# Two attention layers and a mixture of experts: the buffers of the second attention moved, its close dealt out differently among VectorE, ScalarE and GpSimd

## The chip, the cores and the metric

The kernel runs on one core of one Trainium2 chip. The metric is the device time of one execution in microseconds, lower is better. Beside the times there is one execution recorded by the hardware profiler. A core has a matrix engine (TensorE, PE in the profile, with its weight loads as PEld), three elementwise engines (VectorE is DVE, ScalarE is ACT, GpSimd is POOL) and SyncE (SP), which here only starts DMA transfers. Each engine works through its own instructions in order, and they meet at semaphores. PE's clock is granted by a throttle and is shown as a share of full speed.

## What is computed

Four rows of 1024 tokens, 256 numbers each, pass through a first layer of gated attention and a low-rank feed-forward part, then through a second attention and a mixture of experts (8 experts, each takes its 1024 best tokens); each of the four has a normalised input and a normalised output that is added to the stream:

```python
def _L1_attn_ref(x, w_qkv, w_out, b_out, gamma, beta):
    B, S, D, H = (4, 512, 256, 16)
    HD = D // H
    def kernel_func(q, k):
        scores = jnp.einsum('bhqd,bhkd->bhqk', q, k) / jnp.sqrt(jnp.asarray(HD, q.dtype))
        w = jax.nn.relu(scores)
        return w / (jnp.sum(w, axis=-1, keepdims=True) + KERN_EPS)
    ...
    attn = kernel_func(q, k)
    out = jnp.einsum('bhqk,bhkd->bhqd', attn, v)
    out = out.transpose(0, 2, 1, 3).reshape(Bx, Sx, D)
    out = out @ w_out + b_out
    y = x + out
    mu = jnp.mean(y, axis=-1, keepdims=True)
    var = jnp.var(y, axis=-1, keepdims=True)
    return (y - mu) * jax.lax.rsqrt(var + LN_EPS) * gamma + beta
...
x = x + _layernorm(_L0_attn_ref(_layernorm(x, axis=-1), ...), axis=-1)
x = x + _layernorm(_L0_ffn_ref(_layernorm(x, axis=-1), ...), axis=-1)
x = x + _layernorm(_L1_attn_ref(_layernorm(x, axis=-1), ...), axis=-1)
x = x + _layernorm(_L1_ffn_ref(_layernorm(x, axis=-1), ...), axis=-1)
```

The change concerns the second attention, and the end of the first layer where it hands over.

## The kernel before

**Stages.** The first layer (gated attention with its feed-forward part) takes lines 481 to 1080. The tokens are eight blocks `t` of 512 (half rows), each of four tiles of 128 (`NJ`). `add_normalized` gives the steps that normalise a block's result `y` and add it to the residual `xs[t]`; its `apply` runs on ScalarE (L577) and ends with an add on GpSimd (L588). During the last block of this stage, row 0 of the second attention is already projected. The second attention is lines 1090 to 1638, and the mixture of experts follows.

**Score steps.** The second attention is a hand-written loop over rows `b`, half rows `qh`, four groups `g` of four heads, and eight key tiles `kt`: 256 steps. `scores` issues eight matmuls for four heads: two into single PSUM tiles (`s`, three buffers, shared with the side work) and two into a pair tile (`d`, two buffers). ScalarE applies relu to the two singles (L1493), VectorE to the pair (L1498), into a tile `w` of SBUF with three buffers. In the last half row, which is worked in two halves, ScalarE takes the pair in every fourth step (`all_on_act`, L1496). `weigh` (L1510) multiplies the `w` of the step before the last by the values, one step in a loop iteration, accumulating into `po`. When a group ends, VectorE transposes `po` into `turned` (L1563), and every second group `divide` normalises by the sum of weights (L1243 to L1253).

**Side work.** Everything else is cut into `Part`s. Each has needs (other parts, each with an age in steps that must have passed), an estimate of what it costs VectorE, ScalarE and TensorE, and sits in one of two lists. `beside` holds pieces with PE work: projections of the next row (pk, pq, pv), out projections (`pt`, L1274), transposes, gates. One is taken per step, placed ahead of or after the value matmuls. `rest` holds the elementwise parts; `go_on` deals as many as fit. For this, `late` estimates how far each engine is behind: a part adds its cost less the TensorE time that it brings, and every step subtracts an allowance (0.4 us for VectorE, 0.53 for ScalarE); a part is dealt when `late` plus its cost stays within `MOST`. GpSimd has no such estimate. The order of PE, DVE and ACT instructions is that in which this planner issues them (`manual_schedule`).

**The close of a block.** `close` runs after a half row's last group. Per pair of tiles, `project_out` makes `pt` and VectorE adds the residual (L1284) into `y`. Per tile: `stats_y` (statistics on VectorE, then rs and ms on GpSimd, L1113 to L1118), `affine` on GpSimd (three operations: L1122, L1290, L1291), statistics of the result, `shift` on ScalarE (L1295), `add` on VectorE (L1300), statistics again, and `token_rows` (GpSimd L1122 and SP DMAs). `shift` and `add` apply the outer normalisation. The next row's `normalize` (tags `a`) and the projections' last additions lie beside this.

**Buffers.** The pools of the stage are opened in the order `l1a` (work tiles: y, h, hg, oT, ...), `l1w` (the three w tiles), and lie on SBUF space which the first layer's pools have left: the w tiles lie over a work buffer of the first layer, the one that the last block's `y` uses.

**Queues.** Projected q and k go as high and low parts through DRAM: SP stores them (`q_d<-wh`, `q_d<-parts`, `k_d<-parts`), GpSimd's queue loads them back in another layout (L370 kT, L377 q). The parts are built in a list of room tiles that `next_parts` hands out in turn.

Of the kernel before, what the change touches and what calls it, by code (L numbers as in the profile page):

```python
# [74 lines left out]
def kernel(  # L75
# [146 lines left out]
    with ExitStack() as st1:  # L222
# [358 lines left out]
        def add_normalized(tag, t, y):  # L581

            r, stats, scales, shift = stats_steps(tag, y)

            def apply(i0):
                apply_on_act(y(), y(), r, i0)
                if i0:
                    nc.gpsimd.tensor_tensor(xs[t], xs[t], y(), ALU.add)  # L588

            gap = POW if t < NB - 1 else 2.0  # L590
            return [*stats, (0.0, scales), (gap, shift), (0.5, lambda: apply(0)), (0.0, lambda: apply(2))]

# [176 lines left out]
        def first_parts():  # L769

            room = iter(
                [[wh[:, c, i * TB : (i + 1) * TB] for i in range(2)] for c in range(DC)]
                + [[wk.tile([P, TB], F32, tag=tag, name="part", bufs=1) for tag in ("qk", "head3")]]
            )
            kept = list(room)

            def next_parts():
                kept.append(kept.pop(0))
                return kept[-1]

            return next_parts
# [14 lines left out]

        state = {}

        def attend(d, then=None):
# [290 lines left out]
    with ExitStack() as st3:  # L1090

        wk = st3.enter_context(tc.tile_pool(name="l1a", bufs=2))
        wts = st3.enter_context(tc.tile_pool(name="l1w", bufs=3))
        ps = st3.enter_context(tc.tile_pool(name="l1a_ps", bufs=1, space=PSUM))
# [11 lines left out]

        def scale_of(tag, src):

            st = small.tile([P, 6], F32, tag=f"st{tag}", name=f"st{tag}")
            mv = small.tile([P, 2], F32, tag=f"mv{tag}", name=f"mv{tag}")  # L1110
            ve = small.tile([P, 1], F32, tag=f"ve{tag}", name=f"ve{tag}")
            rs = small.tile([P, 1], F32, tag=f"rs{tag}", name=f"rs{tag}")
            nc.vector.bn_stats(st, src)  # L1113
            nc.vector.bn_aggr(mv, st)
            nc.vector.tensor_scalar(ve, mv[:, 1:2], EPS, None, ALU.add)  # L1115
            ms = small.tile([P, 1], F32, tag=f"ms{tag}", name=f"ms{tag}")
            nc.gpsimd.tensor_tensor(rs, ve, mhalf[:, 0:1], ALU.pow)  # L1117
            nc.gpsimd.tensor_scalar(ms, mv[:, 0:1], rs, -1.0, ALU.mult, ALU.mult)  # L1118
            return rs, ms
# [5 lines left out]
        class Part:  # L1125
# [4 lines left out]

            def __init__(self, do, needs=(), vector=0.0, scalar=0.0, tensor=0.0, when=None):
                self.do, self.needs, self.when = do, needs, when
                self.takes, self.tensor = (vector, scalar), tensor
                self.at = None
# [12 lines left out]

        STATS = {"vector": 0.72}

# [17 lines left out]
        def normalize(row, b, k):  # L1167

            h, x = row["h"][k], xs[b * BPB + k]

            def stats(i):
                return scale_of("a", x[:, i, :])

            def apply(i, rs, ms):
                scaled(h[:, i, :], x[:, i, :], rs, ms)

            return by_tile((stats, 0, STATS), (apply, 1, {}))

# [83 lines left out]
        def close(t, h, oT, tiles, at_end):  # L1262
# [3 lines left out]
            def new_y():  # L1266
                nonlocal y
                y = wk.tile([P, NJ, D], F32, tag="y", name="y", bufs=1)
                last_use["y"] = [] if at_end else [parts[4, i] for i in tiles]

# [14 lines left out]
            def stats_y(i):  # L1285
                return scale_of("b", y[:, i, :])

            def affine(i, rs, ms):
                scaled(y[:, i, :], y[:, i, :], rs, ms)
                nc.gpsimd.tensor_tensor(y[:, i, :], y[:, i, :], gam, ALU.mult)  # L1290
                nc.gpsimd.tensor_tensor(y[:, i, :], y[:, i, :], bet, ALU.add)  # L1291

# [142 lines left out]
            if at_end:  # L1435
                return [at_once]
            steps = (
                (stats_y, 0, STATS), (affine, 1, {}), (lambda i: scale_of("c", y[:, i, :]), 2, STATS),
                (shift, 1, {"scalar": 0.5}), (add, 1, {"vector": 0.48}), (stats_x, 0, STATS),
                (token_rows_and_on, 1, {}),  # L1440
            )
            parts = by_tile(*steps, tiles=tiles)
            outs, turns = [], []
            for i in tiles[1::2]:
# [3 lines left out]
                for k in (i - 1, i):  # L1448
                    parts[0, k].needs.append((outs[-1], 0))
                turns.append(  # L1450
                    Part(
                        lambda i=i: turn_gating(i - 1), [(parts[6, i], 2), *((x, 0) for x in turns[-1:])],
                        tensor=0.53, scalar=0.59,
                    )
                )
            outs[0].when = lambda: done(last_use["y"])
            parts[6, tiles[0]].when = lambda: done(last_use["hg"])
            turns[0].when = may_turn
# [8 lines left out]

        def all_on_act(row, halves, kt):

            return halves > 1 and kt // halves % 4 == 1  # L1470

        def scores(row, qh, q2, halves, g, kt):

# [18 lines left out]
            for j, sc in enumerate(singles):  # L1492
                nc.scalar.activation(w[:, j, :], sc, AF.Relu)  # L1493
            if all_on_act(row, halves, kt):

# [26 lines left out]

        late, MOST = [0.0, 0.0], (0.8, 0.2)

# [5 lines left out]

        def next_piece():

            for part in beside:
                if part.ready():
                    beside.remove(part)
                    take(part)
                    return

# [39 lines left out]

        def go_on_with_oldest():

            at = waiting.pop(0)
            if fresh[0]:
                next_piece()
            finish(*at)
            _, _, _, _, halves, g, kt, _ = at
            ended = kt == KT - halves
            if ended:
                late[0] += 0.65 / halves
            elif not fresh[0]:
                next_piece()  # L1590
            fresh[0] = ended

        for b in range(B):
            after = open_row(last=b + 2 == B) if b + 1 < B else None
            for qh in range(BPB):
# [13 lines left out]
                for q2 in range(halves):  # L1609
                    for g in range(NG):  # L1610
                        for kt in range(0, KT, halves):
                            w = scores(row, qh, q2, halves, g, kt)
                            waiting.append((row, b, qh, q2, halves, g, kt, w))
                            Part.now += 1
                            step = kt // halves
                            if step == 1 and g % 2 == 0:
                                if g == 0 and q2 == 0:
                                    fetch_queries(row, qh, 1)
                                elif g and halves == 1:
                                    fetch_queries(*((row, 1) if qh == 0 else (after, 0)), 0)  # L1620
                            on_act = 1.03 if all_on_act(row, halves, kt) else 0.0
                            for i, us in enumerate((0.4 + 1.2 * (on_act > 0), 0.53 - on_act)):
                                late[i] -= us
                            if len(waiting) > 2:
                                go_on_with_oldest()
                            go_on()
# [4 lines left out]
        while beside or rest:  # L1631
            Part.now += 1
            assert Part.now < 2000
            late[:] = [-2.0, -2.0]
            next_piece()
            go_on()
# [562 lines left out]
```

## Time and profile before

| what | value |
|---|---|
| median of 3 runs | 1552.57 us (1549.29 to 1552.65) |
| the profiled execution | 1552.29 us, its span 1550.5 us |
| mean granted TensorE clock | 0.975 |
| first layer, 0 to 421 us | PE busy 408.8, DVE 237.4, ACT 184.0, POOL 120.7 |
| second attention, 421 to 1011.5 us | PE busy 561.1 of 590.5, DVE 461.0, ACT 335.0, POOL 226.0 |
| experts, 1028 to 1550.5 us | PE busy 490.5 of 522.5, DVE 217.9, ACT 109.8, POOL 199.8 |
| relu of two singles, L1493 | 512 of 595 ns |
| relu of the pair on VectorE, L1498 | 248 of 1216 ns |
| relu of the pair on ScalarE, L1496 | 8 of 1031 ns |
| affine on GpSimd, per tile | L1122 552 ns, L1290 748, L1291 727 |
| fused two-input on VectorE, L1300 | 30 of 476 ns |

A busy time is the sum of an engine's instructions in a stretch. In a group's line the first number after the bar is busy time, the second the mean of one instruction in ns, then the idle time of the engine just before them with what ended it. In a timeline a line is start, duration, engine, line and operation, and in brackets the idle time before it and who released it. In a table of windows the columns are the stretch, its length, then busy time (and count) of PE, PEld, DVE, ACT and POOL, the granted clock, the DMA share and GB/s.

### The profile page before, as it was taken

The page shows a single profiled execution, that of the slowest core. Times are in us where ns is not written, and L with a number is a line of the kernel's source. Part 1 is how long each engine was busy: PE and PEld are TensorE (multiplying, and loading weights), DVE is VectorE, ACT ScalarE, POOL GpSimd, SP SyncE. Part 2 cuts the span into 40 slices and gives each one's busy share as a digit, 9 for nine tenths or more (in the row PEclk, how much of TensorE's full clock was granted, in tenths as well). Part 3 has the DMA queues.
Part 4 walks back from the last instruction along what each step waited for, and adds up shares of the span by engine and source line. Part 5 has one row for each costly group of instructions (what it writes and reads, how often), then busy time and mean ns, then how long its engine had stood idle before and what let it go on. Part 6 is the DMA issues. An engine that isn't in the chain of part 4 may idle for free. (4 is left out here: it accounts for less than half of the span.)

```text
span 1550.5 us, 24225 instructions
## 1 busy us (share of the span) xinstructions
PE 1474.1 (95%) x9286; PEld 789.5 (51%) x9286; DVE 928.5 (60%) x2130; ACT 636.4 (41%) x1109; POOL 549.6 (35%) x731
## 2 busy tenths in 40 slices
PE   8999999999799999999999889959999999999996
PEld 4666666666432323332323224526656765675674
DVE  5455665556467788777877878875545632222145
ACT  4244445543455555645554656722122112112142
POOL 4122333223321336333633244412425233342554
PEclk9999999999899999999999999979999999999998
DMA  9400000004313331532243211151324233233364
GB/s 216 126 1 1 1 1 0 1 1 150 112 52 123 89 110 56 157 108 90 69 143 111 91 34 54 32 164 32 79 42 114 55 73 85 59 77 77 65 166 119
DMA packets 91885, 121.58 MB, mean 78 GB/s; under 512 B 24925, under 2 KB 64250, under 8 KB 91642
## 3 DMA queue, kind: packets, MB, share of 16 engines
q1 hardware_dynamic: 70000, 73.09, 15.2%
q0 software_dynamic: 21712, 46.94, 13.2%
q8 instruction: 73, 1.20, 0.3%
q14 instruction: 42, 0.34, 0.1%
q10 hardware_dynamic: 58, 0.01, 0.0%
HBM read 66.90 MB, written 53.12 MB: 77 GB/s over the span
## 5 line engine op out<-in xcount | busy, mean ns | idle before, releaser
L1493 ACT ACTIVATE w<-sc 128x512 f32<-128x512 f32 x512 | 277.7, 595 | 162.0 <-ACT w L1493 71.0
L1498 DVE TENSOR_SCALAR w<-sc 128x1024 f32<-128x1024 f32 x248 | 300.3, 1216 | 62.2 <-PE sc L1484 49.7
L1510 PE MATMUL po<-w,vaug 128*17 128x512 f32 (+1 forms) x2304 | 275.4, 561 | 6.2 <-DVE turned L1563 6.2
L2074 PE MATMUL ph<-xT,w 128*128 128x512 f32 (+1 forms) x544 | 229.6, 574 | 0.3 <-DVE xT L2057 0.3
L2091 PE MATMUL py<-w,hid 128*128 128x256 f32 x1024 | 229.7, 380 | 0.0
L2081 ACT ACTIVATE hid<-ph,mb 128x512 f32<-128x512 f32 (+1 forms) x136 | 89.9, 662 | 340.2 <-PE ph L2074 246.7
L1484 PE MATMUL sc<-q,kT 32*128 32x512 f32 (+1 forms) x2304 | 199.9, 421 | 23.5 <-ACT w L1493 22.2
L2091 PEld LDWEIGHTS py<-w,hid 128*128 128x128 f32 x1024 | 191.7, 190 | 31.7 <-issue 6.7
L1484 PEld LDWEIGHTS sc<-q,kT 32*128 32x128 f32 x2304 | 90.1, 187 | 209.3 <-ACT w L1493 146.3
L2112 POOL DMA_INDIRECT acc_d<-y,idx x56 | 88.5, 1580 | 226.0 <-DVE y L2111 112.0
L2074 PEld LDWEIGHTS ph<-xT,w 128*128 128x128 f32 x544 | 99.7, 190 | 107.2 <-issue 98.4
L2110 DVE TENSOR_TENSOR y<-py,mb 128x256 f32<-128x256 f32 x56 | 23.5, 419 | 127.0 <-PE py L2091 113.1
L1510 PEld LDWEIGHTS po<-w,vaug 128*17 128x17 f32 x2304 | 42.0, 96 | 103.6 <-issue 74.9
L1882 POOL DMA_INDIRECT got<-tok_d,idx x64 | 66.2, 1034 | 62.5 <-DVE counts L1716 24.5
L2057 DVE COPY xT<-tp 128x512 f32<-128x512 f32 (+1 forms) x34 | 22.2, 659 | 71.7 <-PE tp L2052 64.1
L716 PE MATMUL pg<-nT,wh 128*128 128x512 f32 x128 | 61.3, 611 | 1.5 <-ACT nT L655 1.4
L838 PE MATMUL py<-wo,oT 128*128 128x256 f32 x256 | 61.9, 385 | 0.0
L732 PE MATMUL pv<-wh,nT 128*128 128x512 f32 x128 | 59.7, 592 | 0.0
L838 PEld LDWEIGHTS py<-wo,oT 128*128 128x128 f32 x256 | 47.2, 190 | 17.2 <-issue 9.6
L588 POOL TENSOR_TENSOR x<-x,y 128x1024 f32<-128x1024 f32 x14 | 32.9, 2350 | 59.9 <-ACT y L577 59.8
L1117 POOL TENSOR_TENSOR rsg<-veg,mhalf 128x1 f32<-128x1 f32 x30 | 16.6, 552 | 98.6 <-DVE veg L1115 98.5
L903 ACT ACTIVATE hid<-ph,vec 128x512 f32<-128x512 f32 x64 | 39.8, 685 | 27.5 <-PE ph L894 27.3
(303 smaller groups left out, 2060.6 us busy)
## 6 DMA issues: line engine op xcount, KB each, us to landing
q<-q_d POOLq DMA_DIRECT2D x16, 1024.0 KB
w<-in_L_ffn_W_dram SPq DMA_DIRECT2D x16, 1024.0 KB
q_d<-parts SPq DMA_DIRECT2D x48, 256.0 KB
kT<-k_d POOLq DMA_DIRECT2D x16, 512.0 KB
k_d<-parts SPq DMA_DIRECT2D x24, 256.0 KB
acc_d<-logits SPq DMA_DIRECT2D x8, 512.0 KB
q_d<-wh SPq DMA_DIRECT2D x16, 256.0 KB
tok_d<-hg SPq DMA_DIRECT2D x32, 128.0 KB
```

Of the source, the lines that this page charges most:

```text
L716: nc.tensor.matmul(pg, lhsT=wh[:, c, HID + e * P : HID + (e + 1) * P], rhs=d["nT"][:, c, :], start=(c == 0), stop=(c == DC - 1),)
L732: nc.tensor.matmul(pv, lhsT=d["nT"][:, c, i * P : (i + 1) * P], rhs=wh[:, c, 0:HID], start=(c == 0), stop=(c == DC - 1),)
L838: nc.tensor.matmul(py, lhsT=d["oT"][:, e, :], rhs=wo[:, e, :], start=(e == 0), stop=(e == EC - 1))
L1484: nc.tensor.matmul(sc[:, m * n : (m + 1) * n], lhsT=row["kT"][t][rows, r, (kt + m) * P : (kt + m + 1) * P], rhs=row["q"][qh, t][rows, r, p ...
L1493: nc.scalar.activation(w[:, j, :], sc, AF.Relu)
L1498: nc.vector.tensor_scalar(w[:, 2:4, :], pair, 0.0, None, ALU.max)
L1510: nc.tensor.matmul(po[32 * j : 32 * j + HD + 1, weighed(halves, r)], lhsT=row["v"][:, kt + m, HQ * t + 4 * r + j, :], rhs=w[:, j, m * n : ...
L1882: return nc.gpsimd.indirect_dma_start(out=dst, out_offset=None, in_=rows[:, :], in_offset=self.at_chunk(c), bounds_check=NT - 1, oob_is_er ...
L2074: nc.tensor.matmul(ph, lhsT=w1[:, c, f * P : (f + 1) * P], rhs=xT[u][:, c, h * n : (h + 1) * n], start=(c == 0), stop=(c == DC - 1),)
L2081: nc.scalar.activation(hid[:, f, h * n : (h + 1) * n], ph, AF.Gelu, bias=mb1[:, e * FC + f : e * FC + f + 1])
L2091: nc.tensor.matmul(py, lhsT=hid[:, f, i * P : (i + 1) * P], rhs=w2[:, f, :], start=(f == 0), stop=(f == FC - 1),)
L2112: scatter = nc.gpsimd.indirect_dma_start(out=acc_d[:, :], out_offset=lists[e].at_chunk(k), in_=y, in_offset=None, bounds_check=NT - 1, oob ...
```

## The change

Four things are edited.

1. **Buffers.** The pool of the w tiles is opened ahead of that of the work tiles, so the w tiles take the first addresses, where weights of the first layer lay. So that the room of the parts isn't needed longer, `next_parts` hands out its room twice and then takes tiles "h" of the next row (`next_hs`), which `open_row` uses afterwards. The last block of the first layer is applied on GpSimd by four scalings and the add (`apply_on_pool`).
2. **The close.** `stats_y` no longer makes ms. `centre` on VectorE computes (y - mean) * gam in one instruction, and `affine` is one more on VectorE, y * rs + bet; in the last row `affine` stays on GpSimd as two. `shift`, the tile's `apply` and `token_rows` must be two steps behind what they need instead of one.
3. **The planner.** `late` and `MOST` have a third entry for GpSimd, and parts carry a `pool` cost. The piece for a step is chosen before its scores are issued. When a group's end is one or two steps off, one piece that could be done is kept back.
4. **The score pair.** ScalarE takes it in every step whose piece holds PE for more than 1.5 us, and in one of eight steps of a group in the last row (one of four in the half steps).

Counted in the two instruction orders: ACT pair relus go from 8 to 63 and VectorE's from 248 to 193; VectorE gets 30 centres and 24 affines; GpSimd loses 30 scaled y, 30 msb, 30 multiplies by gam and 24 adds of bet, and gets 10 scalings. The matmuls are the same in number.

```diff
@@ add_normalized
-            gap = POW if t < NB - 1 else 2.0
-            return [*stats, (0.0, scales), (gap, shift), (0.5, lambda: apply(0)), (0.0, lambda: apply(2))]
+            def apply_on_pool():
+                for i in range(NJ):
+                    nc.gpsimd.tensor_scalar(
+                        y()[:, i, :], y()[:, i, :], r["mv"][:, i, 0:1], r["rs"][:, i : i + 1], ALU.subtract, ALU.mult
+                    )
+                nc.gpsimd.tensor_tensor(xs[t], xs[t], y(), ALU.add)
+
+            if t == NB - 1:
+                return [*stats, (0.0, scales), (0.0, apply_on_pool)]
+            return [*stats, (0.0, scales), (POW, shift), (0.5, lambda: apply(0)), (0.0, lambda: apply(2))]
@@ first_parts
-            kept = list(room)
+            kept = 2 * list(room)
 
             def next_parts():
-                kept.append(kept.pop(0))
-                return kept[-1]
+                if kept:
+                    return kept.pop(0)
+                next_hs.append(act4("h"))
+                part = next_hs[-1].rearrange("p j d -> p (j d)")
+                return part[:, 0:TB], part[:, TB : 2 * TB]
@@ pools of the second attention
+        wts = st3.enter_context(tc.tile_pool(name="l1w", bufs=3))
         wk = st3.enter_context(tc.tile_pool(name="l1a", bufs=2))
-        wts = st3.enter_context(tc.tile_pool(name="l1w", bufs=3))
@@ normalize
-            return by_tile((stats, 0, STATS), (apply, 1, {}))
+            return by_tile((stats, 0, STATS), (apply, 2, {"pool": 0.6}))
@@ close
             def stats_y(i):
-                return scale_of("b", y[:, i, :])
-
-            def affine(i, rs, ms):
-                scaled(y[:, i, :], y[:, i, :], rs, ms)
-                nc.gpsimd.tensor_tensor(y[:, i, :], y[:, i, :], gam, ALU.mult)
-                nc.gpsimd.tensor_tensor(y[:, i, :], y[:, i, :], bet, ALU.add)
+                return scale_of("b", y[:, i, :], False)
+
+            def centre(i, mean, rs):
+                nc.vector.scalar_tensor_tensor(y[:, i, :], y[:, i, :], mean, gam, ALU.subtract, ALU.mult)
+                return (rs,)
+
+            def affine(i, rs):
+                if at_last:
+                    nc.gpsimd.tensor_scalar(y[:, i, :], y[:, i, :], rs, None, ALU.mult)
+                    nc.gpsimd.tensor_tensor(y[:, i, :], y[:, i, :], bet, ALU.add)
+                else:
+                    nc.vector.scalar_tensor_tensor(y[:, i, :], y[:, i, :], rs, bet, ALU.mult, ALU.add)
...
             steps = (
-                (stats_y, 0, STATS), (affine, 1, {}), (lambda i: scale_of("c", y[:, i, :]), 2, STATS),
-                (shift, 1, {"scalar": 0.5}), (add, 1, {"vector": 0.48}), (stats_x, 0, STATS),
-                (token_rows_and_on, 1, {}),
+                (stats_y, 0, STATS), (centre, 0, {"vector": 0.48}), (affine, 1, {"pool": 1.4} if at_last else {"vector": 0.49}),
+                (lambda i: scale_of("c", y[:, i, :]), int(at_last), STATS), (shift, 2, {"scalar": 0.5}),
+                (add, 1, {"vector": 0.48}), (stats_x, 0, STATS), (token_rows_and_on, 2, {"pool": 0.6}),
             )
@@ planner
-        late, MOST = [0.0, 0.0], (0.8, 0.2)
+        late, MOST = [0.0, 0.0, 0.0], (0.8, 0.2, 0.4)
-        def next_piece():
-
-            for part in beside:
-                if part.ready():
-                    beside.remove(part)
-                    take(part)
-                    return
+        def next_piece(keep=0):
+
+            could = [part for part in beside if part.ready()]
+            return could[0] if len(could) > keep else None
...
+        def piece_for(at):
+
+            soon_ends = at[4] == 1 and 1 < KT - at[6] <= 3
+            return next_piece(1 if soon_ends and not fresh[0] else 0)
@@ loop over score steps
-                            w = scores(row, qh, q2, halves, g, kt)
+                            Part.now += 1
+                            piece = piece_for(waiting[0]) if len(waiting) > 1 else None
+                            on_act = piece is not None and piece.tensor > 1.5
+                            on_act = on_act or row["last"] and kt // halves % (8 // halves) == 4 // halves
+                            w = scores(row, qh, q2, halves, g, kt, on_act)
...
-                            on_act = 1.03 if all_on_act(row, halves, kt) else 0.0
-                            for i, us in enumerate((0.4 + 1.2 * (on_act > 0), 0.53 - on_act)):
+                            for i, us in enumerate((1.62, -0.5, 1.62) if on_act else (0.4, 0.53, 1.62)):
                                 late[i] -= us
```

## The prediction

> **What bounds the kernel now.** First the page: busy time, the 40 slices and the chain that ended last.
>
> ```profile
> PE 1474.1 (95%) x9286; PEld 789.5 (51%) x9286; DVE 928.5 (60%) x2130; ACT 636.4 (41%) x1109; POOL 549.6 (35%) x731
> PE   8999999999799999999999889959999999999996
> PE 31%; DVE 2%; issue 1%; POOL 1%; DMA 0%; ACT 0%; POOLq 0%; DVEq 0%; ACTq 0%
> ```
>
> TensorE is the bound, and time can only come from its 5% of idle and from matmuls at a slow clock. The second attention is the stretch 421.1 to 1011.5 us (first L1484 score matmuls to the last close). Its ideal: 256 score steps of 1.653 us (starts 488.0, 489.65 in the timeline) = 423.2, 51 long pieces beside them at 1.92 = 97.9, 26 transposes at 0.59 = 15.3, 7 gates at 0.96 = 6.7: 543.1 us, an estimate from those rows. Measured 590.4: 47 us are lost here. Second, the windows tell where:
>
> ```profile
> 425.00:450.00 25.00, 21.45 (x177) 6.81 (x178) 17.64 (x25) 14.31 (x27) 10.61 (x17) 0.82 0.07 28
> 550.00:575.00 25.00, 21.26 (x188) 5.45 (x192) 20.21 (x29) 15.29 (x30) 7.02 (x15) 0.93 0.25 73
> 600.00:625.00 25.00, 24.73 (x188) 9.51 (x182) 22.85 (x51) 14.52 (x29) 20.28 (x37) 1.00 0.38 117
> 900.00:925.00 25.00, 20.26 (x180) 5.78 (x180) 17.80 (x30) 12.55 (x25) 11.89 (x23) 0.93 0.15 44
> ```
>
> PE is the first busy number, the granted clock comes third from the end. Most windows look like the third; six (also at 700, 850 and 950) lose 2 to 5 us and clock besides. Third, the groups and the waits say on whom:
>
> ```profile
> L1484 PE MATMUL sc<-q,kT 32*128 32x512 f32 (+1 forms) x2304 | 199.9, 421 | 23.5 <-ACT w L1493 22.2 <-ACT vaug L441 1.0 <-DVE w L1498 0.2
> L1295 ACT ACTIVATE x<-x,msc 128x256 f32<-128x256 f32 x30 | 15.3, 510 | 26.4 <-POOL msc L1118 26.4
> DVE w L1498 <- POOL x L588: 4.6, 1, 4.6
> ```
>
> PE waits for ScalarE's relu, ScalarE for GpSimd. Fourth, the timeline at the two kinds of place. At the boundary:
>
> ```profile
> 423.15 2.07 ACT L577 ACTIVATE y<-y,msg,rsg 128x256 f32<-128x256 f32 x4 [2.40 <-DVE msg L571]
> 425.30 2.34 POOL L588 TENSOR_TENSOR x<-x,y 128x1024 f32<-128x1024 f32 x1 [2.44 <-ACT y L577]
> 427.67 1.08 ACT L1493 ACTIVATE w<-sc 128x512 f32<-128x512 f32 x2 [2.45 <-POOL x L588]
> 428.32 1.28 PE L1484 MATMUL sc<-q,kT 32*128 32x512 f32 x8 [6.29 <-ACT w L1493]
> ```
>
> The first relu (w) lies over the first layer's buffer y, which the last residual add still reads; PE stands 6.29 us, then runs slow. And in the middle:
>
> ```profile
> 908.69 0.72 POOL L1291 TENSOR_TENSOR y<-y,bet 128x256 f32<-128x256 f32 x1
> 909.37 0.55 POOL L1117 TENSOR_TENSOR rsc<-vec,mhalf 128x1 f32<-128x1 f32 x1
> 910.02 0.27 POOL L1118 TENSOR_SCALAR msc<-mvc,rsc 128x1 f32<-128x1 f32 x1
> 910.32 0.51 ACT L1295 ACTIVATE x<-x,msc 128x256 f32<-128x256 f32 x1 [6.09 <-POOL msc L1118]
> 910.73 1.06 ACT L1493 ACTIVATE w<-sc 128x512 f32<-128x512 f32 x2
> 911.36 0.90 PE L1484 MATMUL sc<-q,kT 32*128 32x512 f32 x7 [4.38 <-ACT w L1493]
> 912.19 1.91 PE L1510 MATMUL po<-w,vaug 128*17 128x512 f32 x8
> ```
>
> GpSimd is deep in the affine of a close; ScalarE sits in its fixed order at the shift, 6.09 us, with the relu of the next score step queued behind it; PE stops, and its next eight po matmuls take 1.91 us instead of 1.05.
>
> **What the Trainium skill says.** "TensorE: Matmul & The Clock Gate", What's actually happening: an idle window of about 3.4 us, free-running, halves the clock until a busy one has passed. The trace agrees in kind: half-speed po after PE gaps of 1.81 to 4.38 us, none after gaps up to 0.97; between those the trace has none. "GPSIMD Engine Reference", Engine selection: two-input elementwise is about twice as slow there as on VectorE. The trace: 748 ns (L1290) against 476 for VectorE's fused two-input (L1300), 1.6 times. "ScalarE: Activation LUTs", Rules for kernel authors: relu belongs on VectorE. Here it doesn't hold: a 128x1024 relu takes ScalarE 1031 ns (L1496) and VectorE 1216 (L1498); the measurement decides. "Perfetto Trace Analysis", Optimizing Scalar/DVE Operations: a saturated VectorE may hand work to ScalarE. VectorE is 78% busy in this stage (461.0 of 590.5), 91% in the 600 window.
>
> **The change, part by part.**
>
> *1. Boundary* (pools swapped; next half row's parts kept in "h"; last block's apply on GpSimd). The w tiles now lie over the first layer's weights, whose last readers I find at about 416.5 us, before the first score matmuls (421.10). The relu then waits for its scores alone. Scores at 421.1, and with steps of 1.65 and the first w 1.08 later, the fourth step would start near 426.8, where steady running is reached at 434.95 now: gain 8.2 (6.29 of gap, 1.9 of slow matmuls). GpSimd applies the last block itself: four scaled tiles (0.55, as L1122) plus the same 2.34 add, 4.5 against ScalarE's 2.07 + 2.34: 0.1 later, and it gates only row 1's first normalise, taken many steps later: nothing. The hi/lo parts go by the same SP DMA count from another tile: nothing.
>
> *2. Shift stalls.* The five places (PE gap; loss against 1.65 per step, slow matmuls included): 550 (2.71; 4.73), 701 (2.87; 6.15), 853 (3.21; 5.20), 906 (4.38; 6.39), 969 (1.81; 3.67). Sum 26.1. The change takes from GpSimd, per tile of a close, the scaled y (0.55), msb (0.27) and the gam multiply (0.75), and the bet add (0.73) in three rows of four; shift is due two steps after its statistics instead of one, and GpSimd's lateness is now counted before a part is dealt. GpSimd's work per close falls by 4 x 2.30 = 9.2 us; in the last row by 4 x 1.57 less 4 x 0.55 for the new scaling = 4.1. The gaps are all smaller than that, so I take all 26.1; if half of a backlog stayed, the gain here would be 13. Late next is ScalarE's own queue: two relu singles (1.19) + shift 0.51 = 1.70 against a step of 1.65, absorbed over two steps.
>
> *3. VectorE gains.* +30 centre and +24 affine at 0.47 = +25 us; ScalarE takes the score pair in 63 steps instead of 8: -55 x 1.216 = -67 us. Net -42 of 461. ScalarE +55 x 1.03 = +57 on 335 in 590: 66%, no bound on average.
>
> *4. VectorE bursts, the new cost.* Where no long piece runs, the pair of step n must leave its bank (two of them) before step n+2's scores: 2 x 1.65 = 3.3 us, less the relu's 1.2, leaves 2.05 us for what VectorE does ahead of it. Before, the largest burst just fits:
>
> ```profile
> 747.18 0.69 DVE L1284 TENSOR_TENSOR y<-pt,h 128x512 f32<-128x512 f32 x1 [1.24 <-PE pt L1274]
> 747.79 0.42 DVE L1113 BATCH_NORM_STATS2 sta<-x 128x6 f32<-128x256 f32 x1
> 749.27 1.22 DVE L1498 TENSOR_SCALAR w<-sc 128x1024 f32<-128x1024 f32 x1
> ```
>
> y add and two statistics, 0.69 + 2 x 0.70, pair at 749.27. In the changed instruction order I find after the out projections: y add + two statistics + two centres (0.65 + 1.48 + 0.9 = 3.03) ahead of a VectorE pair in closes 0, 2, 4, a delay of about 1.1 and then 0.6 from the two affines: 1.75 each, 5.2; y add + four statistics (3.6) in closes 1 and 3: 1.55 each, 3.1; closes 5 and 7: 1.35 + 1.55 = 2.9. Sum 11.2 us. These gaps of 1.1 to 1.6 fall in the unmeasured band of the clock: from 0 to 2 us each over nine of them (0 to 18). I take 2 in all, since gaps of 0.97 cost nothing. Below nothing is excluded: a burst adds work to VectorE ahead of a fixed deadline.
>
> *5. Small edits.* One piece is kept back for group ends; by the order, group ends with nothing beside them go from 17 to 15 of 35, at 0.4 us (PE po behind DVE turned: 6.2 us in 13 waits): 0.8 gained. At closes 1 and 3 the kT DMA now stands in GpSimd's queue between rsc and msc: up to 0.5 us, within shift's two steps: nothing; if that cover is gone, 1 us. The MoE (1028 us on) has the same instructions: nothing.
>
> Sum: 8.2 + 26.1 + 0.8 - 11.2 - 2 = 21.9 us off the profiled execution's 1552.3: 1530. The median of the runs shown, 1552.57, is 0.3 above it.
>
> **Rivals.**
>
> R1, bursts hidden: VectorE's net -42 us lets it run ahead, and the banks have a slack that I read too tightly. For: the 2.05 limit is from one place. Against: the deadlines are local. Gain 8.2 + 26.1 + 0.8 = 35: 1517.
>
> R2, each burst gap also brings a half-clock window of 2 us: 9 x 2 = 18 more than part 4's 2: gain 35.1 - 11.2 - 18 = 6, 1546. For: 1.81 did it. Against: 1.81 is above all of these.
>
> R3, the change doesn't do what it says at the boundary: w still waits there, for a last DMA or TensorE reader of the weights. Gain 21.9 - 8.2 = 14: 1538. Against: these readers end by 416.5.
>
> R4, slower: VectorE becomes the bound at the closes. One mechanism: each close puts its centres and affines, 4 x 0.96 = 3.84 us, whole on PE, and each brings a slow window as the 701 gap did, 6.15 - 2.87 = 3.3; six closes at 7.1 and 1.5 for the half one: 44 lost against 35.1 gained, 1561. It decides from 35.1 / 7 = 5.0 us per close; I expect 1.6. For: VectorE at 91% in the 600 window. Against: the relief of 67 us lies in the same steps.
>
> **Numbers.** Forecast 0.53 (own range 1522 to 1538), R1 0.24, R2 0.13, R3 0.05, R4 0.05. Predicted 1530. The range 1515 to 1544 takes R1, R3 and part of R2, leaving some 0.15 out. No change means within 0.3% (4.7 us), about what a measurement of this kernel can tell: faster is below 1548. From the cases: R2 above 1548 gives 0.03 to same, R4's lower end 0.01; the rest of R4 is slower. Faster 0.92, same 0.04, slower 0.04.
>
> **What would show it.** First scores and first w apart by about 1 us, no wait on POOL x; no wait of L1295 on msc above 1 us and clock 1.00 in the 550, 700, 850 and 900 windows; instead PE sc waiting for the DVE pair, about 11 us in sum, 1.1 to 1.6 each, in the steps after out projections. Wrong if those waits exceed 2 us each or are absent, if POOL msc is still late in the last row (its bet add stays on GpSimd), or if the MoE moves.

## The result, and the profile after

| what | before | changed |
|---|---|---|
| median | 1552.35 us (1549.29 to 1552.65, 4 runs) | 1529.45 us (1527.22 to 1532.15, 4 runs) |
| ratio | 1 | 0.9858, 95% interval 0.9834 to 0.9881 |
| span of the profiled execution | 1550.5 us | 1525.9 us |
| first score matmul of the second attention at | 421.1 us | 420.1 us |
| from there to its last po matmul | 590.5 us | 567.8 us |
| from there to the first count of the experts (the tail) | 19.1 us | 19.0 us |
| the experts to the end | 519.8 us | 519.0 us |

The span fell by 24.6 us, 22.6 of it between the first score and the last po matmul; 21.9 were forecast in all. The experts are 0.8 us shorter by chance: their instructions are the same and take 518.5 to 520.2 us in all fourteen profiles of this study. The first layer is 1.0 us shorter, but not by its own edits: with these alone it ends at 421.2 us, as before. The last section shows what moves its end.

In those 590.5 us PE was busy for 561.2 and idle for 29.3; in the 567.8 us now it is busy for 550.3 and idle for 17.5. The stretches at half clock in them add up to 30.7 us before and 3.4 now. So about half of the gain is idle time, and the other half is busy time, the matmuls being the same in number.

In the changed kernel the score matmuls are line L1501, po L1527, the singles' relu L1510, the pair on ScalarE L1513 and on VectorE L1515, turned L1583. First its table of windows, at the places that answer to the four shown before (25.00 is the length, then busy time of PE, PEld, DVE, ACT, POOL, then the clock):

```profile
425.00:450.00 25.00, 25.00 (x200) 8.60 (x200) 13.22 (x18) 17.25 (x30) 13.13 (x20) 1.00 0.12 40
540.00:565.00 25.00, 23.14 (x219) 6.12 (x216) 23.07 (x34) 15.98 (x32) 4.74 (x10) 1.00 0.25 86
590.00:615.00 25.00, 23.84 (x176) 9.07 (x168) 20.52 (x53) 17.26 (x30) 13.50 (x25) 1.00 0.30 91
870.00:895.00 25.00, 22.93 (x216) 6.75 (x208) 22.28 (x42) 16.61 (x32) 7.16 (x15) 1.00 0.17 53
```

The stretch after the boundary is full at full clock (25.00 us against 21.45 at 0.82). At the two closes PE is idle for 1.9 and 2.1 us where it was for 3.7 and 4.7, and the clock stays at 1.00. The third window, the one that was nearly full before (24.73), now has 1.2 us of idle time; the stall in it is shown below. The groups and waits of the changed kernel say who is late now:

```profile
L1315 ACT ACTIVATE x<-x,msc 128x256 f32<-128x256 f32 x30 | 15.3, 510 | 0.0
PE po L1527 <- DVE turned L1583: 11.3, 15, 2.9
PE sc L1501 <- DVE w L1515: 4.8, 6, 1.2
PE sc L1501 <- ACT w L1510: 1.2, 3, 0.5
```

(In a line of waits: us in all, times, the longest.) ScalarE stood idle for 26.4 us ahead of its shift, behind msc, and now for none; PE's wait for ScalarE's relu fell from 22.2 us to 1.2. In their place PE waits for VectorE: 4.8 us for the pair (0.2 before) and 11.3 for turned. The latter was in the kernel before:

```profile
PE po L1510 <- DVE turned L1563: 6.2, 13, 0.7
```

The boundary in the timeline of the changed kernel (start, duration, then engine and operation):

```profile
420.10 0.93 PE L1501 MATMUL sc<-q,kT 32*128 32x512 f32 x9 [0.96 <-ACT vaug L441]
420.88 3.50 ACT L1510 ACTIVATE w<-sc 128x512 f32<-128x512 f32 x6 [1.12 <-PE sc L1501]
421.53 0.99 PE L1501 MATMUL sc<-q,kT 32*128 32x512 f32 x8 [0.50 <-ACT w L1510]
421.97 4.85 POOL L592 TENSOR_SCALAR y<-y,mvg,rsg 128x256 f32<-128x256 f32 x4
426.91 2.40 POOL L595 TENSOR_TENSOR x<-x,y 128x1024 f32<-128x1024 f32 x1
```

The first relu starts 0.78 us after its scores (6.57 before), while GpSimd still applies the last block (4.85 + 2.40 us, where 4.5 were forecast), and no matmul waits for it.

A new stall, in the timeline after an out projection (the PE pt matmuls before 587.45):

```profile
587.56 0.69 DVE L1298 TENSOR_TENSOR y<-pt,h 128x512 f32<-128x512 f32 x1 [2.53 <-PE pt L1288]
590.38 0.42 DVE L1125 BATCH_NORM_STATS2 stb<-y 128x6 f32<-128x256 f32 x1
590.75 0.50 PE L1501 MATMUL sc<-q,kT 32*128 32x512 f32 x2
591.14 1.23 DVE L1515 TENSOR_SCALAR w<-sc 128x1024 f32<-128x1024 f32 x1
592.42 0.73 PE L1501 MATMUL sc<-q,kT 32*128 32x512 f32 x6 [1.17 <-DVE w L1515]
593.08 1.05 PE L1527 MATMUL po<-w,vaug 128*17 128x512 f32 x8
```

y add and four statistics fill VectorE from 587.56 to 591.14, then comes the pair, and the scores two steps on wait for its bank. The bracket says 1.17, but two of the eight matmuls had run before the wait: from their start to the po behind them it takes 2.33 us and in an undisturbed step 0.67 (588.12 less 587.45), so the loss is 1.66.

### The profile page after: what moved, and what is told of

It is laid out like the page before. It is cut to its first block, busy times and chain, and to the rows that moved or that the text cites. A ratio compares the mean times of both kernels' runs of the same rounds, so it can differ in the third digit from the quotient of the medians.

```text
span 1525.9 us, 24163 instructions
## 1 busy us (share of the span) xinstructions
PE 1462.9 (96%) x9286; PEld 787.0 (52%) x9286; DVE 887.4 (58%) x2128; ACT 685.0 (45%) x1160; POOL 495.7 (32%) x627
## 5 line engine op out<-in xcount | busy, mean ns | idle before, releaser
L1510 ACT ACTIVATE w<-sc 128x512 f32<-128x512 f32 x512 | 278.0, 595 | 141.9 <-ACT w L1510 60.4
L1527 PE MATMUL po<-w,vaug 128*17 128x512 f32 (+1 forms) x2304 | 270.1, 552 | 11.6 <-DVE turned L1583 11.3
L1515 DVE TENSOR_SCALAR w<-sc 128x1024 f32<-128x1024 f32 x193 | 234.4, 1219 | 43.2 <-PE sc L1501 37.1
L1501 PE MATMUL sc<-q,kT 32*128 32x512 f32 (+1 forms) x2304 | 195.2, 413 | 6.9 <-DVE w L1515 4.8
L1501 PEld LDWEIGHTS sc<-q,kT 32*128 32x128 f32 x2304 | 88.4, 184 | 182.4 <-ACT w L1510 122.6
L1527 PEld LDWEIGHTS po<-w,vaug 128*17 128x17 f32 x2304 | 41.8, 95 | 104.8 <-issue 74.2
L1513 ACT ACTIVATE w<-sc 128x1024 f32<-128x1024 f32 x63 | 65.1, 1033 | 0.0
L2086 DVE COPY xT<-tp 128x512 f32<-128x512 f32 (+1 forms) x34 | 22.2, 659 | 71.7 <-PE tp L2081 63.9
L850 PEld LDWEIGHTS py<-wo,oT 128*128 128x128 f32 x256 | 47.2, 190 | 17.1 <-issue 9.6
```

Source lines behind the costliest of these rows:

```text
L850: nc.tensor.matmul(py, lhsT=d["oT"][:, e, :], rhs=wo[:, e, :], start=(e == 0), stop=(e == EC - 1))
L1501: nc.tensor.matmul(sc[:, m * n : (m + 1) * n], lhsT=row["kT"][t][rows, r, (kt + m) * P : (kt + m + 1) * P], rhs=row["q"][qh, t][rows, r, p ...
L1513: nc.scalar.activation(w[:, 2:4, :], pair, AF.Relu)
L1515: nc.vector.tensor_scalar(w[:, 2:4, :], pair, 0.0, None, ALU.max)
L1527: nc.tensor.matmul(po[32 * j : 32 * j + HD + 1, weighed(halves, r)], lhsT=row["v"][:, kt + m, HQ * t + 4 * r + j, :], rhs=w[:, j, m * n : ...
```

## The experiments

Each was timed in three rounds (the last in five) beside the kernel before. "Stage" is the time from the first score to the last po matmul, "tail" from there to the experts' first count, both in the profiled execution. Each ratio is to the runs of the kernel before that lay beside. Where two ratios are subtracted below, both intervals together leave some 4 to 5 us either way.

| kernel | ratio, interval | stage | tail |
|---|---|---|---|
| before | 1 | 590.5 | 19.1 |
| changed | 0.9858 (0.9834 to 0.9881) | 567.8 | 19.0 |
| boundary alone | 0.9958 (0.9943 to 0.9974) | 584.0 | 19.5 |
| changed without boundary | 0.9896 (0.9879 to 0.9912) | 573.7 | 20.3 |
| shift later alone | 0.9958 (0.9941 to 0.9974) | 577.8 | 23.6 |
| lateness on the kernel before | 0.9934 (0.9918 to 0.9951) | 569.9 | 29.6 |
| changed, affine on GpSimd | 0.9898 (0.9882 to 0.9915) | 576.4 | 18.8 |
| changed, pairs on VectorE | 0.9926 (0.9904 to 0.9949) | 579.7 | 19.2 |
| changed, no piece kept | 1.0019 (1.0008 to 1.0030) | 589.2 | 19.9 |
| changed, pair after out projections | 0.9843 (0.9825 to 0.9860) | 567.2 | 20.0 |
| changed, pair at bare ends | 0.9935 (0.9910 to 0.9960) | 559.9 | 40.4 |
| changed, both pairs | 0.9884 (0.9867 to 0.9900) | 554.8 | 40.2 |
| both pairs, not in the last half row | 0.9809 (0.9792 to 0.9826) | 561.0 | 19.0 |
| both pairs, last half row unplanned | 0.9798 (0.9780 to 0.9816) | 562.9 | 19.5 |

**Boundary alone**: on the kernel before, the pools swapped, the parts in "h", the last block applied on GpSimd.

```diff
+        wts = st3.enter_context(tc.tile_pool(name="l1w", bufs=3))
         wk = st3.enter_context(tc.tile_pool(name="l1a", bufs=2))
-        wts = st3.enter_context(tc.tile_pool(name="l1w", bufs=3))
...
+            if t == NB - 1:
+                return [*stats, (0.0, scales), (0.0, apply_on_pool)]
```

> The kernel before with the buffer part of the change alone (pools swapped, parts in h, last block applied on GpSimd). Theory: the boundary is worth 7.7 us (lead of the changed kernel over the one before at the eighth score step, 8.7, less the 1.0 us by which its first layer was shorter) and is independent of the rest: 1544 to 1545 us, no wait of the first relu on POOL x L588, and the five shift stalls stand as before (PE gaps of 1.8 to 4.4 us, 15 us in sum). Rival: the earlier start moves the order of GpSimd and the shift stalls change too: a time below 1539 or above 1549.

1544.32 us against 1550.42 in the runs beside it: 6.1 gained, 4.0 to 8.8 by the interval. The five shift stalls stand where they stood (2.75, 2.83, 3.08, 4.39 and 1.82 us). The boundary is a part of its own.

**The changed kernel without it**, the same edit undone.

> The changed kernel without its buffer part. Theory: the gap of about 6 us before the second scores is back with a slow stretch after it, all else as in the changed kernel: 1537 us (1529.4 + 7.7), no shift stall. Rival: the freed end of the first layer is hidden or made up later, because the second attention then has slack: under 1533.

1534.6 us: 1.0% below the kernel before against 1.4, so the boundary is worth 5.9 us here too (0.9896 - 0.9858 = 0.0038 of 1552). The 6.30 us gap is back. The rival, that it would be made up later, isn't borne out: the time is over its 1533, though by less than the interval. The size is below the 7.7 that the two traces had shown.

**Shift later alone**, on the kernel before.

```diff
-                (shift, 1, {"scalar": 0.5}), (add, 1, {"vector": 0.48}), (stats_x, 0, STATS),
+                (shift, 2, {"scalar": 0.5}), (add, 1, {"vector": 0.48}), (stats_x, 0, STATS),
```

> The kernel before with one number changed: shift is due two steps after its statistics instead of one. Theory: the five stalls are a GpSimd that is late by 1.8 to 4.4 us, so one step of 1.65 shortens each by about that: gaps from 15 us to 7, with fewer slow windows, 1538 to 1543. Rival: ScalarE meets the same late msc, since the planner then piles other parts on GpSimd: 1548 or more.

Its gaps at the closes are 0.84, 0.84, 0.69, 2.79 and 1.83: 7.0 us, as expected, and the stage is 12.7 us shorter, for one number. The time, 1544.43, is a little over the range; the tail took 4.5 us back.

**Lateness on the kernel before**: GpSimd counted, its parts priced (the affine at 1.4 us, though its three operations take 2.0), shift, apply and token rows two steps behind; affine on GpSimd, buffers and pairs as before.

```diff
-                (stats_y, 0, STATS), (affine, 1, {}), (lambda i: scale_of("c", y[:, i, :]), 2, STATS),
-                (shift, 1, {"scalar": 0.5}), ...
+                (stats_y, 0, STATS), (affine, 1, {"pool": 1.4}), (lambda i: scale_of("c", y[:, i, :]), 2, STATS),
+                (shift, 2, {"scalar": 0.5}), ...
-        late, MOST = [0.0, 0.0], (0.8, 0.2)
+        late, MOST = [0.0, 0.0, 0.0], (0.8, 0.2, 0.4)
```

> The kernel before with the planner's part of the change alone: GpSimd's lateness counted, prices for its parts, shift, apply and token rows two steps behind; affine stays on GpSimd as three operations (priced 1.4 us), ScalarE gets no more pairs, the buffers stay. Theory, after the run with affine on GpSimd: the count and the step cure most of the five stalls by themselves: gaps on ScalarE under 4 us in sum, 1532 to 1540. Rival: without the centres and affines moved to VectorE GpSimd is late all the same: 1545 or more.

1540.45 us. The stage is 20.6 us shorter than before, though every affine still runs on GpSimd; PE's gaps behind ScalarE's relu at the closes are 1.29, 0.79 and 0.27. But GpSimd's last parts now come after the scores (before, the last affine began 10 us ahead of the end of po), and 10.5 us return in the tail, 7.1 of them as waits of the transposes for GpSimd:

```profile
988.03 0.72 POOL L1291 TENSOR_TENSOR y<-y,bet 128x256 f32<-128x256 f32 x1
994.29 0.48 PE L1329 MATMUL tpg<-ident,hg 128*128 128x128 f32 x1 [6.00 <-POOL hg L1122]
```

The last po matmul of this kernel ends at 987.4; an affine of a close is still under way then, and PE stands 6.00 us for the token rows (hg) that are made after it.

**Affine on GpSimd in the changed kernel**, three operations, priced at their 2.0 us. Two more numbers differ from the changed kernel: the second statistics are due two steps after the affine, as in the kernel before (not at once, or in the last row one step after), and GpSimd's limit is 1.0 instead of 0.4.

```diff
-            def centre(i, mean, rs):
-                nc.vector.scalar_tensor_tensor(y[:, i, :], y[:, i, :], mean, gam, ALU.subtract, ALU.mult)
-                return (rs,)
+            def centre(i, rs, ms):
+                return (rs, ms)
...
+                scaled(y[:, i, :], y[:, i, :], rs, ms)
+                nc.gpsimd.tensor_tensor(y[:, i, :], y[:, i, :], gam, ALU.mult)
+                nc.gpsimd.tensor_tensor(y[:, i, :], y[:, i, :], bet, ALU.add)
...
-                (stats_y, 0, STATS), (centre, 0, {"vector": 0.48}), (affine, 1, {"pool": 1.4} if at_last else {"vector": 0.49}),
-                (lambda i: scale_of("c", y[:, i, :]), int(at_last), STATS), (shift, 2, {"scalar": 0.5}),
+                (stats_y, 0, STATS), (centre, 0, {}), (affine, 1, {"pool": 2.0}),
+                (lambda i: scale_of("c", y[:, i, :]), 2, STATS), (shift, 2, {"scalar": 0.5}),
...
-        late, MOST = [0.0, 0.0, 0.0], (0.8, 0.2, 0.4)
+        late, MOST = [0.0, 0.0, 0.0], (0.8, 0.2, 1.0)
```

> The changed kernel with the affine of the close back on GpSimd (scale, gam, bet, 2.0 us per tile), known to the planner at its full price, ages as in the changed kernel (statistics of y' two steps after it, shift two steps after its statistics). Theory: it was the GpSimd work taken away that cured the shift stalls; then ScalarE's x waits for msc again, PE gaps above 1.5 us at the closes, 1540 us or more. Rival: counting GpSimd's lateness and the later shift suffice: no msc wait above 1 us and, since VectorE loses 25 us and the centres leave its bursts, 1525 to 1531.

1535.15 us, between the two. Waits for msc are back on ScalarE (8.9 us in 7, the longest 2.6), of which 3.6 us reach PE. The stage is 8.6 us longer than the changed one, but PE's idle time in it only 1.7 (19.2 against 17.5): the rest is busy time, with 17.1 us at half clock against 3.4, and 6.8 of the 17.1 lie at the boundary, where they are chance (last section). So the moved affine, with the two numbers that go with it, is worth some 6 us in time (0.0040 of 1552), not the whole of the cure.

**Pairs on VectorE** in the changed plan.

```diff
-                            w = scores(row, qh, q2, halves, g, kt, on_act)
+                            w = scores(row, qh, q2, halves, g, kt, halves > 1 and kt // halves % 4 == 1)
```

> The changed kernel in the same planned order, but with VectorE doing the 55 score pairs that ScalarE had got (ScalarE keeps the 8 of the kernel before). Theory: the pair on ScalarE is what makes room for the centres and affines; VectorE then has 55 x 1.22 = 67 us more in the very steps in which the planner gave it work, about 0.4 us of stall each: 1550 us or more, PE sc waiting for DVE w 15 us or more. Rival: VectorE stands idle ahead of the y add anyway (2.5 us before L1298, waiting for pt), so the pair fits there: under 1536.

1540.39 us, 0.0068 or 10.6 us over the changed kernel: both numbers missed, the truth is between. PE sc waits 9.2 us for VectorE's pair (4.8 in the changed kernel) and 3.6 more for VectorE's parts and y. That the pair fits in part into VectorE's idle time ahead of y add would give such a size; it is argued, not measured.

**No piece kept back.**

```diff
-            return next_piece(1 if soon_ends and not fresh[0] else 0)
+            return next_piece(0)
```

> The changed kernel without keeping one piece back for the ends of groups. Theory: the piece kept back covers an end here and there (0.4 to 0.8 us of PE waiting for turned): PE's waits on DVE turned grow from 11.3 to 13 us or more, 1530 to 1533. Rival: the keeping does nothing or harm (the changed kernel waits longer on turned than the one before, 11.3 against 6.2): 1529 or less.

1555.14 us, slower than before the change. The direction is the theory's, the size isn't near it. The profile is of the fastest of its eleven executions (1547.06), so it shows less than the median lost. Its waits:

```profile
PE po L1527 <- DVE turned L1583: 22.6, 21, 3.7
PE sc L1501 <- DVE w L1515: 6.8, 5, 1.8
```

21 ends wait instead of 15, and for twice the time. At the worst of them in its timeline, a burst and an end fall together:

```profile
729.45 0.47 DVE L1303 SCALAR_TENSOR_TENSOR y<-y,mvb,gam 128x256 f32<-128x256 f32 x1
729.84 1.22 DVE L1515 TENSOR_SCALAR w<-sc 128x1024 f32<-128x1024 f32 x1
731.12 0.73 PE L1501 MATMUL sc<-q,kT 32*128 32x512 f32 x6 [1.54 <-DVE w L1515]
734.28 1.22 DVE L1515 TENSOR_SCALAR w<-sc 128x1024 f32<-128x1024 f32 x1
735.42 0.70 DVE L1583 STREAM_TRANSPOSE turned<-po 128x512 f32<-128x512 f32 x1
736.18 1.05 PE L1527 MATMUL po<-w,vaug 128*17 128x512 f32 x4 [3.74 <-DVE turned L1583]
```

The scores stand 1.54 us for the first pair, then the next group's po 3.74 us for turned, which is behind the second. Another stall has nothing to do with ends of groups; it is a shift stall again:

```profile
760.37 0.75 POOL L370 DMA_DIRECT2D kT<-k_d  x1 [5.46 <-DMA k_d<-parts]
761.47 0.91 ACT L1315 ACTIVATE x<-x,msc 128x256 f32<-128x256 f32 x2 [4.57 <-POOL msc L1132]
762.91 1.71 PE L1501 MATMUL sc<-q,kT 32*128 32x512 f32 x8 [3.07 <-ACT w L1510]
```

GpSimd stands 5.46 us in its order until k is stored and it may load kT; msc comes after that, ScalarE's shift and relu after msc, and PE waits 3.07 us. This is the cover that the prediction spoke of in its part on small edits: in the changed kernel it holds, in this order it is gone. Four half-speed windows, 17 us long together, stand at the four gaps of 2.89 us and more; the changed kernel has one of 3.4 us in this stage. PE's idle time in the stage is 33.6 us against 17.5.

**Pair after out projections**: ScalarE takes it in the step after one (`was_out`), 79 in all.

```diff
-                            w = scores(row, qh, q2, halves, g, kt, on_act)
+                            w = scores(row, qh, q2, halves, g, kt, on_act or was_out[0])
...
-                            for i, us in enumerate((1.62, -0.5, 1.62) if on_act else (0.4, 0.53, 1.62)):
+                            for i, us in enumerate((1.62, -0.5, 1.62) if on_act else (0.4, -0.5 if was_out[0] else 0.53, 1.62)):
...
+                            was_out[0] = piece is not None and piece.takes[0] == 0.69
```

> The changed kernel, with ScalarE taking the score pair also in the step after an out projection (16 pairs more). Theory of the VectorE bursts: y add, statistics and centres stand ahead of VectorE's next pair; without that pair PE's waits of sc on DVE w (4.8 us in six) fall under 1.5, 1525 to 1527. Rival: ScalarE's singles come late instead (PE sc waiting for ACT w, over 3 us more) or the burst delays turned all the same: 1529 or more.

1528.05 us, between the theory's range and the rival's. The waits of sc on the pair fall from 4.8 to 0.4 us, as the theory of the bursts has it. The gain is small and within the intervals: turned then waits behind the same burst (12.3 us).

**Pair at bare ends**, in the steps in which a group ends with no piece beside it, 78 in all, and **both**, 96.

```diff
+                            on_act = on_act or piece is None and len(waiting) > 1 and ends(waiting[0])
```

> The changed kernel, with ScalarE taking the score pair also in the steps in which a group ends with no piece beside it (15 pairs more). Theory: turned is late because VectorE's pair of the newer step stands ahead of it; with that pair on ScalarE the waits of po on DVE turned fall from 11.3 us to 5 or less: 1521 to 1525. Rival: turned waits for the last po matmuls and for its own 0.65 us; the waits stay above 8 us: 1528 or more.

> Both: ScalarE takes the pair after out projections and at bare ends of groups. Theory: the two gains add, as they lie in different steps: 3 + 6 us, 1518 to 1523. Rival: ScalarE (96 pairs now against 63) becomes late and its shift and copies hold PE: above 1526.

The first takes 1539.8 us, the second 1534.14. Both lie in the ranges of the rivals, but for a reason that neither rival names. The waits of po on turned do fall (4.1 us in the first, while those of the scores on the pair rise to 7.6), and with both the stage is 554.8 us, 13 less than the changed one. But the plan now holds the close of block 6 back past the last scores, and in the tail of the second kernel PE waits for it:

```profile
PE tpg L1349 <- POOL hg L1136: 12.2, 6, 5.6
ACT x L1315 <- POOL msc L1132: 4.5, 2, 3.8
```

The tail takes 40 us instead of 19, with 23.4 us of matmuls in it instead of 14.4. So some 9 of the stage's 13 us are work that was only moved, and the waits for GpSimd come on top. The last run below gives ScalarE as many pairs, 96, without telling the planner of those in the last half row, and its tail is 19.5: it is the plan that was late, not the engine. Which count of the plan isn't separated, since that run also grants VectorE 0.4 us instead of 1.62 in the steps with a bare end.

**Both pairs, not in the last half row** (`more` only where `halves == 1`, 91 pairs).

```diff
+                            more = halves == 1 and not on_act and (
+                                was_out[0] or piece is None and len(waiting) > 1 and ends(waiting[0])
+                            )
+                            w = scores(row, qh, q2, halves, g, kt, on_act or more)
```

> The changed kernel with both pairs more for ScalarE (after out projections, at bare ends of groups), but not in the last half row, where the earlier runs of this kind put off the close of block 6 past the end. Theory: it keeps the 8 to 13 us that those gained before the end of the scores and has the tail of the changed kernel: 1516 to 1523. Rival: the work that ScalarE took on early is made up in the last half row, with stalls there: 1526 or more.

1520.45 us, faster than both kernels. PE's waits for turned are 7.8 us, those for the pair 0.4, and the tail is 19.0.

**The same, with the last half row too**, the planner untold there.

```diff
-                            more = halves == 1 and not on_act and (
+                            more = True and not on_act and (
...
-                            for i, us in enumerate((1.62, -0.5, 1.62) if on_act else (0.4, -0.5 if more else 0.53, 1.62)):
+                            for i, us in enumerate((1.62, -0.5, 1.62) if on_act else (0.4, -0.5 if more and halves == 1 else 0.53, 1.62)):
```

> As the run before, and in the last half row ScalarE takes the pair at the same two places, which the planner isn't told of there, so that the plan stays. Theory: the 2.9 us wait of po for turned after the last out projections comes from VectorE's pair behind the burst (y add, four statistics), and with it the half-clock window goes: waits on turned under 5 us, 1515 to 1519. Rival: turned is behind the statistics themselves or ScalarE comes late in the half steps: 1520 or more.

1519.48 us, ratio 0.9798. That is between the ranges of the theory and the rival. The waits for turned are 4.9 us in all, as the theory had it; the one of 2.9 us is 1.76, and the half-clock window after it remains. The intervals of the two kernels overlap, so which is better stays open.

## Why the prediction was right, and where it wasn't

The total, 22 us off, is what was measured (22.9 in the medians). That it came so near is luck in part: the terms missed in both directions, and their measured sizes don't add up to the gain. By its steps:

**Boundary, 8.2.** The place and the mechanism are shown by both runs on it. The size is 5.9 to 6.1 by the medians, with an interval of 4.0 to 8.8 in the run on it alone. The traces say what lies between: counted from the first scores, the lead over the kernel before at the eighth score step is 7.7 us in the changed kernel, whose profile has no half-speed window on the first scores, 6.4 in the boundary alone, which has one of 3.4 us there, and 5.0 in the pair after out projections, which has one of 6.8. The step counted on none.

**Shift stalls, 26.1.** All five are gone, as forecast. The cause that the step named, GpSimd's 9.2 us less per close, is only a part. One step more for shift cuts the gaps at the closes from 15.0 to 7.0 us; counting GpSimd's lateness as well gives a stage 20.6 us shorter with the affine where it was. What the moved affine adds is smaller: with the lateness counted but the affine left on GpSimd, the kernel before has a tail 10.5 us longer, and the changed kernel loses some 6 us in time.

**VectorE's bursts, 11.2.** Right in place; the sum is right in part by luck. The losses, read as above from the start of the disturbed scores to the next po less 0.67, and with 0.26 in the step after where it is also late, are 1.3, 1.35 and 1.34 at closes 0, 2 and 4 (forecast 1.75 each), 1.66 and 1.67 at closes 1 and 3 (1.55), 1.31 at close 5 (1.35), and 2.91 at close 7 (1.55), there as a wait for turned: 11.5 in all. Closes 0, 2 and 4 cost 0.4 us less each than forecast, and close 7 costs 1.4 more and by another wait. The 2.91 us is over the 2 us that the prediction had named as a sign of being wrong, and the waits of the scores on the pair come to 4.8 us in the trace, not 11; read by whole steps these six are 8.6. Moving that one pair to ScalarE takes the waits on it from 4.8 to 0.4 us, which is the experiment for these six; in the time, the gain is within the intervals.

**Clock after the bursts, 2.** One window of 3.4 us at half clock follows the 2.91 us gap, some 1.7 us; none follows the gaps of 1.17 and less. The rival with a window at each gap falls. The trace before could have told some of this: that it has no gap between 0.97 and 1.81 us holds for the score steps, but in the first layer a gap of 1.45 us at 34.31 has no half-speed window after it.

**Small edits, 0.8.** Wrong in sign and in kind. (Waits of GpSimd's queue, put at nothing here, were nothing in this order and 3 us of PE in the order without the piece kept.) Waits for turned grew from 6.2 to 11.3 us, 2.2 of that outside close 7; and the piece kept back, of which only two ends less were counted, carries the plan: without it 25 us are lost (1.0019 - 0.9858 of 1552). An edit of the planner was priced by the waits that it removes in the one order at hand; its worth is what the other order would meet.

Of the rivals, hidden bursts (1517) fall by the losses listed, VectorE as the bound (1561) by the same sum, 1.6 us per close as against 5.0, and the boundary that does nothing by the first run. The step's parts don't sum exactly: 7.7 + 26.1 - 11.5 - 1.7 - 2.2 is 18.4 and the stage gained 22.6; 4 us I couldn't place, and that pieces lie in other steps in the two orders is only a guess at them. What the Trainium skill, "Perfetto Trace Analysis", Optimizing Scalar/DVE Operations, says of handing a saturated VectorE's work to ScalarE held here at a VectorE that was 78% busy in this stage: the 55 pairs are worth 10.6 us, 28 more 7.6 (0.0049).

## What to carry to other kernels

When a hand-ordered plan deals work to in-order engines, count every engine's lateness in it: one uncounted engine stops the others, and a wait placed one step later was the cheapest repair here. Price a burst by what stands ahead of the instruction that frees a bank, and read the loss from the steps around it, since a gap in the middle of a group of matmuls shows only part of it. And look at the tail for each plan: work held back by lateness comes due there, with nothing beside it, and a stage from which matmuls have moved into the tail looks faster than it is.

## What the hardware showed that was not expected

The trace's record of the granted clock changes in units of 3.4 us, and the half-speed stretches last 3.4 us or a multiple of it. The Trainium skill, "TensorE: Matmul & The Clock Gate", What's actually happening, tells of a free-running window of 3413 ns, and the runs agree: it isn't the gap alone that decides. In the first layer PE waits for VectorE at about 396 us in every one of the fourteen profiles, each time for 3.21 to 3.23 us; nine of them have a half-speed stretch of 6.8 us there, the changed kernel's one of 3.4, and four none. Among smaller gaps, one of 1.47 us was followed by a slow window (pair at bare ends), one of 1.81 was not (no piece kept), one of 1.61 was (pairs on VectorE).

The same window may make much of the measurement's spread. In the eight of the twelve trial kernels' profiles that have the stretch of 6.8 us, the second attention starts at 419.9 to 421.4 us; in the four with none it starts at 417.5 to 417.8, though the instructions there are all but the same. The eight have a second one at about 423 us, among the first score steps, of 3.4 to 10.2 us; of the four, only the one with the old boundary has it. So a few us of a single profile's boundary are chance: the changed kernel's profile had 3.4 us at half speed at 397 and none at 423, and its lead of 7.7 us at the boundary is more than the 5.9 to 6.1 of the medians.
